# Running the last feed-forward sublayer inside the steps of the cross attention before it, with float32r halves

## The chip, the cores and the metric

The kernel runs on one core of a Trainium2 chip. A core has five engines with a queue of instructions each: TensorE (PE in the profile; PEld is its loading of the stationary operand), VectorE (DVE), ScalarE (ACT), GpSimd (POOL) and SyncE (SP, which here only issues transfers). They run side by side and wait for each other with semaphores. The metric is the device time of one execution in microseconds; three executions of the kernel before are shown below.

## The reference

A decoder of four layers works on 64 sequences of 64 tokens with 256 channels, 4096 tokens in all. Each layer has three sublayers (self attention, a cross sublayer, a feed-forward), each followed by `x = layernorm(x + sublayer(x))`. The change concerns the last layer:

```python
x = _layernorm(x + _L3_attn_ref(x, ...))        # sublayer 10: 16 heads of 128
x = _layernorm(x + _L3_xattn_ref(x, ctx, ...))  # sublayer 11: 16 query heads, 4 key/value heads
x = _layernorm(x + _L3_ffn_ref(x, w_fc, w_proj))  # sublayer 12

def bitlinear(x, w):
    xn = layer_norm(x)                  # eps 1e-6
    x_hat = clip(xn * 128 / max|xn|, -128 + eps, 128 - eps) * max|xn| / 128
    w_hat = sign(round(w / (mean|w| + eps))) * mean|w|     # ternary weights
    return x_hat @ w_hat.T
ffn(x) = bitlinear(gelu(bitlinear(x, w_fc)), w_proj)       # 256 -> 1024 -> 256
```

The weights of the twelfth sublayer are thus -1, 0 or 1 times one number per matrix.

## The kernel before

All tokens stay in SBUF: eight groups `X[g]` of four tiles (`TG = 4`) of 128 tokens by 256 channels, in float32. Beside them stand eight buffers `CT[g]` of the same size that hold the turned context until the cross attention has used it. Large weights go through a ring of eight buffers. PSUM is divided into banks with names: "mm" (two banks in the attentions; the products "p" come there), "tr" (two banks, for every group of up to four transposes, `transpose4`), "s", "y" and "acc".

Sublayers 10 and 11 are one loop (`l3_attentions`, L1870). Its items are 64 for the self attention and 64 for the cross attention, two (`hb` = 0, 1: half of the heads) for each of the 32 token tiles. A step `i` works on item `i` and finishes earlier ones: it projects the queries of item i, turns the queries and keys of item i-1 and makes its scores, takes the softmax rows of item i-2 through a transpose to the product with the values, and multiplies item i-3 by the output matrix. The order of PE's instructions is that of the code (`manual_schedule` for PE). The order on the other engines and the issue of transfers is set by a planner, which simulates the program with its own costs. In the cross attention the order of PE in a step is: turned query 0 of item i-1, query 0, turned key, turned query 1, outputs of item i-3 (L2274, 16 instructions), scores of item i-1 (L2223, 32), turned softmax rows of item i-2, query 1, and for some tiles the values' projection, then values of item i-2 (L2255). On even steps of 14 of the 32 tiles keys and values are loaded from memory, where they have been written earlier (`ContextRows`); for the other 18 they are projected in the step.

The tiles of x are turned (tokens to the free axis) for the projections by whole groups: four transposes and one copy of 512 columns for each half of the channels (`transposed`, `rows`, L2287). The row's end of the cross attention (`tile_normalized`, L360 to L367) finishes x tile by tile, three items after its queries.

Sublayer 12 (`l3_ffn`) is a stage of its own behind the loop. Its weights are made ternary ahead of it (`ternary`, L2315 to L2326, on DVE and POOL), during the cross attention. The normalised and clipped rows of a group (`l3_quantized`, L2337 to L2354) go to `CT[g]`; the first two groups are made near the end of the cross attention. Per tile: `hidden` (L2398, four float32 products of 512 columns, then Gelu L2402 on ACT and the normalisation of 1024 columns on DVE, POOL and ACT), `turned` (eight transposes, two copies, L2412), `output` (L2419, eight float32 products of 256 columns, then the sum with x and the last layernorm). The transposition of a tile stands two to three steps behind its hidden products. The 32 tiles are stored at the end of the program (L479), each once it is final.

Gelu, Exp and Silu need different tables in ACT; where the function changes to one whose table is not loaded, the program has an instruction ACT_TABLE_LOAD.

## Time and profile before

| what | value |
|---|---|
| time, median of 3 runs | 4254.79 us |
| lowest and highest of them | 4251.92 and 4256.56 us |
| span of the profiled execution, first to last instruction | 4250.0 us |
| mean granted TensorE clock | 0.986 |
| scores of the self attention, L2004, first and last start | 1903.2 and 3149.3 us |
| scores of the cross attention, L2223, first and last start | 3174.2 and 3949.7 us |
| last product of the cross attention's output, end | 3963.8 us |
| feed-forward, from there to the end | 286.2 us |

The profile's own execution has no time besides its span; the median of the runs is 4.8 us above that span. In a line of groups the columns are the source line, the engine, the operation, what is written and read with its form, the number of instructions, their busy time in us, the mean of one in ns, and the idle time of the engine just before them with what ended it. The durations of PE's products are longer than the distance of their starts, because they are pipelined; the distance of starts is the pace.

### The profile page before, as it was taken

To read this page: it belongs to the slowest core of one execution; us is meant where nothing else is said; L and a number is where in the kernel's file an instruction comes from. 1 tells how busy PE (TensorE), PEld (TensorE's weight loads), DVE (VectorE), ACT (ScalarE), POOL (GpSimd) and SP (SyncE) were. 2 spreads that over 40 slices of the span, in tenths; PEclk is the share of its full clock that TensorE was granted. 3 is DMA by queue.
4 is the path that set the end of the run, shared out by engine and by line. 5 is a ranking of instruction groups with operands and counts; after the bars stand their busy time and mean duration, and the time that the engine had idled before them with its cause. 6 is when DMAs were issued, how large, how long until landed. Compare 5 with 4: busy or idle time off the path is not lost.

```text
span 4250.0 us, 74130 instructions
## 1 busy us (share of the span) xinstructions
PE 4051.5 (95%) x28788; PEld 2618.4 (62%) x28808; DVE 3042.7 (72%) x6107; ACT 2106.4 (50%) x3863; POOL 1506.3 (35%) x1553
## 2 busy tenths in 40 slices
PE   8889999989998999989999999999999999999998
PEld 5645556666675555546666666666656666666666
DVE  6844548888685688877777777777766777777786
ACT  5555635767634577544444444444433444444443
POOL 4511112242341111115555555555544444444111
PEclk9989999999999999999999999999999999999999
DMA  2200002333300000031111111111131100000000
GB/s 81 73 21 10 1 26 69 72 84 71 82 1 12 1 1 1 10 132 28 26 31 26 26 31 26 26 30 27 26 102 28 26 23 21 23 23 16 11 16 18
DMA packets 108294, 144.00 MB, mean 34 GB/s; under 512 B 15844, under 2 KB 73380, under 8 KB 106536
## 3 DMA queue, kind: packets, MB, share of 16 engines
q1 hardware_dynamic: 106984, 137.69, 12.7%
q8 instruction: 228, 3.74, 0.4%
q10 hardware_dynamic: 960, 1.57, 0.2%
q14 instruction: 122, 1.00, 0.1%
HBM read 70.25 MB, written 26.76 MB: 23 GB/s over the span
## 4 chain that ended last, share of the span: by engine, by line
PE 65%; DVE 15%; ACT 6%; POOL 4%; issue 3%; DMA 1%; SPq 0%; POOLq 0%; ACTq 0%; DVEq 0%
PE p L1777 19%; PE acc L2066 5%; PE acc L2274 4%; PE sq L1208 3%; PE ret L1247 2%; PE qT L319 2%; PE acc L1396 2%; POOL rstd L313 2%; DVE bnst L339 2%; PE gate L911 2%; DVE mc L1213 2%; PE gate L1592 2%; PE sk L1211 2%; PE s L2004 2%; PE up L911 2%
## 5 line engine op out<-in xcount | busy, mean ns | idle before, releaser
L313 POOL TENSOR_TENSOR rstd<-rstd,neg_half 128x1 f32<-128x1 f32 (+1 forms) x195 | 157.9, 810 | 653.1 <-DVE rstd L311 585.2
L313 POOL TENSOR_TENSOR hrq<-hrq,neg_half 128x4 f32<-128x4 f32 x256 | 258.7, 1011 | 300.7 <-DVE hrq L311 283.9
L1213 DVE TENSOR_REDUCE mc<-sq 128x2 f32<-128x512 f32 x512 | 317.1, 682 | 63.9 <-PE sk L1211 63.7
L1219 ACT ACTIVATE e<-sk 128x512 f32<-128x512 f32 x512 | 265.5, 608 | 112.1 <-PE sk L1211 111.5
L1208 PE MATMUL sq<-l1x 32*128 32x256 f32 x2048 | 275.2, 407 | 4.9 <-DVE z L1094 3.1
L1777 PE MATMUL p<-l3a_wq,xt 128*128 128x512 f32 x512 | 243.8, 599 | 11.2 <-DVE v L300 9.9
L313 POOL TENSOR_TENSOR hrk<-hrk,neg_half 128x4 f32<-128x4 f32 x160 | 188.2, 1176 | 185.8 <-DVE hrk L311 181.0
L1211 PE MATMUL sk<-l1x 32*128 32x256 f32 x2048 | 252.9, 392 | 0.0
L1777 PE MATMUL p<-l3a_wk,xt 128*128 128x512 f32 x512 | 247.1, 605 | 0.0
L1208 PEld LDWEIGHTS sq<-l1x 32*128 32x128 f32 x2048 | 208.3, 195 | 58.8 <-issue 23.6
L1777 PE MATMUL p<-l3x_wq,xt 128*128 128x512 f32 x512 | 242.3, 596 | 0.3 <-DVE k L2168 0.3
L1777 PE MATMUL p<-l3a_wv,xt 128*128 128x512 f32 x512 | 233.9, 599 | 0.4 <-ACT y L94 0.4
L2274 PE MATMUL acc<-l3x_wo,yt 128*128 128x256 f32 x1024 | 232.4, 380 | 1.6 <-DVE yt L300 1.0
L2066 PE MATMUL acc<-l3a_wproj,yt 128*128 128x256 f32 x1024 | 232.0, 379 | 0.5 <-DVE yt L300 0.5
L2066 PEld LDWEIGHTS acc<-l3a_wproj,yt 128*128 128x128 f32 x1024 | 194.2, 190 | 53.7 <-issue 29.2
L2274 PEld LDWEIGHTS acc<-l3x_wo,yt 128*128 128x128 f32 x1024 | 190.5, 190 | 33.9 <-issue 7.7
L1211 PEld LDWEIGHTS sk<-l1x 32*128 32x128 f32 x2048 | 188.5, 187 | 7.3 <-issue 2.9
L2237 POOL TENSOR_TENSOR s<-s,smx 128x512 f32<-128x512 f32 x64 | 66.9, 1046 | 333.8 <-DVE smx L2236 319.8
L319 PEld LDWEIGHTS qT<-ident,q 128*128 128x128 f32 x1024 | 121.9, 141 | 95.9 <-issue 75.2
L2050 POOL TENSOR_TENSOR hry<-hry,neg_half 128x8 f32<-128x8 f32 x64 | 106.2, 1659 | 183.4 <-DVE hry L2046 183.4
L319 PE MATMUL qT<-ident,q 128*128 128x128 f32 x1024 | 157.4, 277 | 3.3 <-ACT qT L2208 2.4
L1247 PE MATMUL ret<-e,vt 128*32 128x256 f32 x2048 | 140.6, 390 | 18.2 <-DVE mc L1213 17.2
(415 smaller groups left out, 10209.4 us busy)
## 6 DMA issues: line engine op xcount, KB each, us to landing
vs<-v SPq DMA_DIRECT2D x308, 128.0 KB
l3x_kv<-kv SPq DMA_DIRECT2D x28, 256.0 KB
x<-in_x SPq DMA_DIRECT2D x8, 512.0 KB
ct<-in_ctxT SPq DMA_DIRECT2D x8, 512.0 KB
cn<-in_ctx SPq DMA_DIRECT2D x8, 512.0 KB
l1x<-in_ctx SPq DMA_DIRECT2D x128, 32.0 KB
l1x_x<-x SPq DMA_DIRECT2D x8, 512.0 KB
l1x<-l1x_x SPq DMA_DIRECT2D x128, 32.0 KB
```

Source lines behind the costliest of these rows:

```text
L313: nc.gpsimd.tensor_tensor(out, out, self.neg_half[:, :n], ALU.pow)
L319: self.nc.tensor.transpose(ps[:, j * P : (j + 1) * P], blk, self.ident)
L911: nc.tensor.matmul(ps[:n], w[:, c, h0 : h0 + n], xt[:, c, :], start=c == 0, stop=c == 1)
L1208: nc.tensor.matmul(ps[:, n, :], x_[rows, j, part], c_[rows, j, :], start=True, stop=True)
L1211: nc.tensor.matmul(ps[:, n, :], c_[rows, j, part], x_[rows, j, :], start=True, stop=True)
L1213: nc.vector.tensor_reduce(mc[new % 2][:, ra + k, 2 * j : 2 * j + 2], ps, AX.X, ALU.max, negate=True)
L1219: nc.scalar.activation(es[rb + k], ps, AF.Exp, scale=scale)
L1247: nc.tensor.matmul(ret[32 * r : 32 * r + 32, :], vt[i % 2][:, lc, 4 * r + j, :], es[r][:, lc, :], start=lc == 0, stop=lc == 1,)
L1777: self.nc.tensor.matmul(ps, lhs(c), w(c, cols), start=c == 0, stop=c == 1 and bias is None)
L2050: nc.gpsimd.tensor_tensor(r, r, self.neg_half[:, :8], ALU.pow)
L2066: nc.tensor.matmul(acc[:, :D], yts[h % 2][:, h // 2, :], wp[n // 8][:, (n % 8) * D : (n % 8 + 1) * D], start=n == 0, stop=n == 15,)
L2274: nc.tensor.matmul(acc[:, :D], yts[h % 2][:, h // 2, :], w.o[n // 8][:, (n % 8) * D : (n % 8 + 1) * D], start=n == 0, stop=n == 15,)
```

## The change

A new class `L3Ffn` holds the twelfth sublayer as six pieces per tile, and each piece is put into a step of the loop over sublayers 10 and 11. Hidden products of tile k stand in step `max(n + 2k + 7, n + 25 + 4k // 3)` with n = 64: 89, 90, 91, 93, 94, 95, ... up to 127 for k = 28, and then 129, 131 and 133. The rows of a tile are normalised two steps earlier and turned one step earlier; the scales of the hidden rows follow in the same step, their transposition stands at the end of the next one, the output product and the store in the one after it. The loop runs to step 135 instead of 130. The stage `l3_ffn` and its helpers are gone.

The moving rows are split: after a transpose, ACT copies the PSUM bank into a float32r tile (`hi`) and DVE writes the difference into a second one (`lo`). The ternary weights are float32r as well. A float32 product becomes two float32r products that add up in PSUM. The statistics of the hidden rows come from accumulators of Gelu and of two Square activations in place of DVE's batch statistics. Dividing by the maximum and clipping becomes one clip between -max and max (`limited`). The last layernorm is applied on ACT. The weights are loaded in pieces, twice each (for the mean size and for the sign), in steps 71 to 78, two pieces a step. Hidden rows lie in `CT[0]` and `CT[1]`, small rows in `CT[2]`. The hidden and output products take the banks of "mm", and their transposes those of "tr".

Independently of this, x is turned tile by tile in both attentions: two transposes and one ACT copy of 256 columns at the end of every even step, for the tile that starts two steps later.

```diff
+class L3Ffn:
+    def __init__(self, dec, wk, n):
+        tiles = range(dec.n_groups * TG)
+        first = [max(n + 2 * k + 7, n + 25 + 4 * k // 3) for k in tiles]
+        self.last = first[-1] + 2
+        for k, at in zip(tiles, first):
+            for stage, later in (
+                ("rows", -2), ("rows_turned", -1), ("hidden", 0), ("scales", 0), ("turned", 1), ("output", 2)
+            ):
+                self.events.setdefault((stage, at + later), []).append(lambda s=stage, k=k: getattr(self, s)(k))
+        for i, part in enumerate(self.ternary("l3f_wfc", 0) + self.ternary("l3f_wproj", 1)):
+            self.events.setdefault(("weights", n + 7 + i // 2), []).append(part)
...
+        def size(i):
+            nc.vector.tensor_reduce(col[:, i : i + 1], piece(i), AX.X, ALU.add, apply_absolute_value=True)
...
+        def sign(i):
+            raw, thr, out = piece(i), st["thr"], st["w"][:, i * 512 : (i + 1) * 512]
+            nc.vector.tensor_scalar(out, raw, thr[:, 1:2], None, ALU.is_lt)
+            nc.vector.scalar_tensor_tensor(out, raw, thr[:, 0:1], out.bitcast(F32), ALU.is_gt, ALU.subtract)
...
+    def limited(self, x):
+        am = self.dec.small(2, "am")
+        nc.vector.tensor_reduce(am[:, 0:1], x, AX.X, ALU.max, apply_absolute_value=True)
+        nc.vector.tensor_scalar_mul(am[:, 1:2], am[:, 0:1], -1.0)
+        nc.vector.tensor_scalar(x, x, am[:, 0:1], am[:, 1:2], ALU.min, ALU.max)
+    def standard(self, out, x, eps):
...
+        nc.vector.bn_stats(st, x)
+        nc.vector.bn_aggr(mv, st)
+        dec.rsqrt(r, mv[:, 1:2], 1.0, eps)
+        nc.vector.scalar_tensor_tensor(b, mv[:, 0:1], -1.0, r, ALU.mult, ALU.mult)
+        nc.scalar.activation(out, x, AF.Identity, bias=b, scale=r)
+    def halves(self, hi, lo, ps):
+        self.nc.scalar.copy(hi, ps)
+        self.nc.vector.tensor_tensor(lo, ps, hi.bitcast(F32), ALU.subtract)
+    def rows(self, k):
+        self.standard(out, self.dec.X[g][:, t, :], 1e-6)
+        self.limited(out)
+    def rows_turned(self, k):
+        ps = self.dec.transpose4([rows[:, c * P : (c + 1) * P] for c in range(2)], "xt")
+        xs = [wk.tile([P, 2, P], F32R, tag=n, name=n, bufs=1) for n in ("xhi", "xlo")]
+        self.halves(*(x.rearrange("p c n -> p (c n)") for x in xs), ps[:, :D])
+    def hidden(self, k):
+        for i in range(2):
+            ps, cols = dec.bank("h", bufs=2), slice(i * 512, (i + 1) * 512)
+            for c in range(2):
+                for j, x in enumerate(xs):
+                    nc.tensor.matmul(ps, x[:, c, :], w[:, c, cols], start=c + j == 0, stop=c + j == 2)
+            nc.scalar.activation(h[:, cols], ps, AF.Gelu, scale=self.gammas[0], accum_out=col[:, i : i + 1])
+    def scales(self, k):
+        nc.vector.tensor_scalar(nb, col[:, 0:1], col[:, 1:2], -1.0 / self.HID, ALU.add, ALU.mult)
+        for i in range(2):
+            sq = self.wk.tile([P, 512], F32, tag="sq", name="sq")
+            nc.scalar.activation(
+                sq, h[:, i * 512 : (i + 1) * 512], AF.Square, bias=nb, accum_out=ss[:, i : i + 1]
+            )
+        nc.vector.tensor_scalar(r, ss[:, 0:1], ss[:, 1:2], 1e-6 * self.HID, ALU.add, ALU.add)
+        nc.gpsimd.tensor_tensor(r, r, dec.neg_half[:, :1], ALU.pow)
+        nc.vector.tensor_tensor(b, nb, r, ALU.mult)
+        nc.scalar.activation(h, h, AF.Identity, bias=b, scale=r)
+        self.limited(h)
+    def turned(self, k):
+        for i in range(2):
+            ps = self.dec.transpose4([h[:, (4 * i + j) * P : (4 * i + j + 1) * P] for j in range(4)], "ht")
...
+            self.halves(*(x.rearrange("p j t -> p (j t)") for x in hs), ps)
+    def output(self, k):
+        ps = dec.bank("o", bufs=2)
+        for j in range(8):
+            for m in range(2):
+                nc.tensor.matmul(
+                    ps[:, :D], hts[j // 4][m][:, j % 4, :], w[:, j, :], start=j + m == 0, stop=j + m == 8
+                )
+        nc.vector.scalar_tensor_tensor(z, ps[:, :D], self.gammas[1], x, ALU.mult, ALU.add)
+        self.standard(x, z, 1e-5)
+        nc.sync.dma_start(out=dec.out[at : at + P, :], in_=x)
...
@@ l3_attentions @@
-            for i in range(2 * n + 3):
+            for i in range(ffn.last + 1):
...
                     do(0, "query", 0)
+                    ffn.run("output", i)
                     do(1, "key_turned")
                     do(1, "turn", 1)
-
+                    ffn.run("hidden", i)
...
                 while self.row_ends:
                     self.row_ends.pop(0)()
-                if i in (n - 3, n - 2):
-                    two.rows(0, i - n + 3)
+                for stage in ("scales", "weights", "turned", "rows_turned", "rows"):
+                    ffn.run(stage, i)
+                if i % 2 == 0 and i + 2 < 2 * n:
+                    which, j = at(i + 2)
+                    which.rows(j // 2)
...
+    def tile_turned(self, wk, k):
+        ps = self.transpose4([self.X[g][:, t, c * P : (c + 1) * P] for c in range(2)], "xt")
+        xt = wk.tile([P, 2, P], F32, tag="xt", name="xt", bufs=3)
+        self.nc.scalar.copy(xt, ps[:, :D].rearrange("p (c n) -> p c n", c=2))
```

## The prediction

> **What bounds the kernel now.** I read the page first, then the same busy times by stretch, then single rows. The page's head:
>
> ```profile
> PE 4051.5 (95%) x28788; PEld 2618.4 (62%) x28808; DVE 3042.7 (72%) x6107; ACT 2106.4 (50%) x3863; POOL 1506.3 (35%) x1553
> ```
>
> PE leads, but "busy" has modelled ends, so I use busy times only to see where PE stops. The change touches the end of the program: the eleventh sublayer (cross attention, steps 64 to 130 of the loop at L1870, scores at L2223 from 3174.2 to 3949.7 us) and the twelfth (feed-forward, after the last L2274 product at 3963.8 us). The same view by stretch, four attention steps and then the feed-forward (columns: stretch, its length, busy us of PE, PEld, DVE, ACT, POOL):
>
> ```profile
> 3696.41:3744.19 47.78, 47.65 (x358) 32.95 (x357) 35.42 (x68) 19.90 (x35) 20.09 (x21) 1.00 0.10 23
> 3990.00:4230.00 240.00, 224.00 (x940) 153.32 (x938) 189.03 (x531) 110.51 (x170) 40.03 (x60) 1.00 0.05 16
> ```
>
> In the attention PE never stops and four steps (two token tiles) take 47.75 us. DVE has 12 us idle in them, ACT and POOL 28 each. In the feed-forward nobody is full: PE 93%, DVE 79%. Its groups in the stretch 3990 to 4225 (us busy, mean ns, idle before):
>
> ```profile
> L2419 PE MATMUL o<-l3f_wproj,ht 128*128 128x256 f32 x443 | 101.9, 381 | 5.2 <-ACT ht L2412 5.2
> L2348 DVE TENSOR_REDUCE am<-hn 128x1 f32<-128x1024 f32 x28 | 34.1, 1218 | 21.5 <-ACT hn L2342 21.1
> L2342 ACT ACTIVATE hn<-h,nmr,rstd 128x1024 f32<-128x1024 f32 x27 | 33.5, 1240 | 83.2 <-DVE nmr L2337 82.8 <-DVE bnmv L342 0.4
> ```
>
> The idle of ACT is spent on DVE and that of DVE on ACT: one tile's normalisation runs back and forth. The chain of work that ended last agrees: in that stretch it goes through DVE, POOL and ACT, hardly through PE. So 286.2 us (3963.8 to 4250.0) are paid for 32 tiles, 8.9 us each. Pace of PE and price of an ACT table, from the timeline:
>
> ```profile
> 1162.72 0.59 PE L1378 MATMUL gate<-xt,l_signs 128*128 128x512 bf16 x2
> 1163.16 0.59 PE L1378 MATMUL up<-xt,l_signs 128*128 128x512 bf16 x2
> ...
> 4158.80 1.04 PE L319 MATMUL ht<-ident,hn 128*128 128x128 f32 x8
> 4159.67 3.60 PE L2398 MATMUL h<-l3f_wfc,xt 128*128 128x512 f32 x8
> 4163.11 3.62 PE L2419 MATMUL o<-l3f_wproj,ht 128*128 128x256 f32 x16
> ...
> 1502.87 0.47 ACT L1564 ACTIVATE eq<-qk,ss 128x256 f32<-128x256 f32 x1
> 1503.24 0.47 ACT L1566 ACTIVATE wv<-qk,ss 128x256 f32<-128x256 f32 x1
> 1503.73 1.28 ACT L1596 ACT_TABLE_LOAD   x1
> 1505.02 0.60 ACT L1596 ACTIVATE hid<-gate 128x512 f32<-128x512 f32 x1
> ```
>
> A bf16 product of 512 columns is one instruction, 0.216 us from start to start (two in 0.44). One f32 product is two instructions (8 for 4 products in L2398) of (3.60-0.59)/7 = 0.43 us: 0.86 us, four times as much. A transpose costs 0.11.
>
> **The change, part by part.**
>
> *Removed:* the feed-forward as a stage of its own, 286.2 us, with its wait for the attention's last rows and its back-and-forth per tile.
>
> *PE work put into the attention.* Per tile: hidden, 4 products as two float32r halves = 8 instructions of 512 columns; output, 8 products = 16 of 256; transposes 8+2. No row shows float32r. Bounds: the bf16 pace (0.216 per 512 columns, one instruction) and the f32 pace (0.86). I take bf16, because the operand is cut into two halves and each needs no second part, which is what makes f32 two instructions. Then 8 x 0.216 + 16 x 0.108 + 10 x 0.11 = 4.5 us, against 3.6 + 3.6 + 1.3 = 8.5 now. The weight loads of transposes follow each other at the same 0.11, so they do not hold 256 columns back (0.108). The page "FP8 and Floating Point Precision" (TensorE Precision Notes) says that true FP32 takes four passes and that a reduced form reads FP32 cut to FP22; the trace agrees on the factor four, and no run here shows the reduced form; by one pass the estimate is the same 4.5 us.
>
> *The pace of the new steps.* The schedule `first` hides hidden(k) at step 89 + 4k/3, so 3 tiles per 4 steps until step 127: tiles 0 to 28. Floor by PE: 47.75 + 3 x 4.5 = 61.2 us per 4 steps.
>
> Other engines in those 4 steps. DVE per tile: rows 0.40 + 0.17 + 0.15 + 0.16 + about 0.36 (maximum over 256, half of L2145's 0.67) + 0.14 + 0.35; halves of the rows 0.42 (L360); scales 0.15 x 3 + 1.22 + 0.14 + 0.74; halves of the hidden rows 2 x 0.68 (L2168, PSUM, 512); output 0.47 + 0.42 + 0.17 + 0.15 + 0.16: sum 7.5. Group sums overlap: 213 us of them are 189.0 busy in the stretch, so 6.7. DVE: 35.4 + 3 x 6.7 = 55.5, fits under 61.2. ACT per tile: 0.60 + 0.37 + 2 x 0.69 + 2 x 0.63 + 4 x 0.20 (read-outs of accumulators, as L1557) + 1.24 + 2 x 0.58 + 0.60 = 7.4. Gelu and Exp now alternate; Silu and Exp do in the trace, with 1.28 us at every change: two per tile, 2.6. ACT: 19.9 + 3 x 10.0 = 50. POOL: 20 + 3 x 3 x 0.62 = 25.6.
>
> Against this the page "ScalarE: Activation LUTs" (Table sets: the hidden batching unit; What ACT_TABLE_LOAD costs) speaks: batch by set, for a switch costs about 2.66 us, 1.28 and a drain. Here the load starts 0.02 us after the activation before it ends and the next begins at its end, so 1.28 is what this trace supports. By the page ACT would be at 58 of some 67, still under PE.
>
> *Waits added on PE.* They come from order, not from load. At the end of a step `turned` fills both "tr" banks; `rows_turned`, the xt transposes or the next step's qT need the first one again. It comes free only after ACT's copy (0.58) and then DVE's subtraction (0.68), with some 0.15 us between engines: 1.4 us, less 0.43 in which the second bank is filled. That is 1.0 us per tile with both queues empty. DVE has a backlog at the end of a step: at 3774.4 the yt products are done and DVE finishes its copy only at 3775.9, the hrq reduction at 3776.6, so 1 us more. Behind the waiting transpose all of PE's next step waits. Per 4 steps: three such pairs, 3 x 2.0; two refills more by rows and xt, 0.25 each: 6.5 us. Bounds: 0 (queues empty, PE finds the bank free) and 14 (nine bank uses, each behind 1.5 us of backlog). The shared "p" banks add nothing in my sum: hidden falls on steps 1, 2, 3 of four, where query 1 comes 5 us later, behind out, scores and pt.
>
> So 67.7 us per 4 steps, 20 more than now, 6.65 per tile; 29 tiles: **+193 us**.
>
> *The tail.* The last three tiles stand at steps 129, 131 and 133 with PE nearly idle: a chain of latencies. From the last L2274 product: row's end 2.8 (3963.8 to 3966.6 now); behind it tile 30's output, hidden, scales (squares 1.3, pow 0.6, identity 1.24, maximum 1.22, clip 0.9, hops) and turning, to about 18; tile 31's hidden 1.7, gelu 1.5, scales 6.3, turning 0.9, copies 1.4, output 1.8, z to x 2.5 (4244.9 to 4247.4 now), store 2.5: **+36 us**, bounds 28 and 45.
>
> *With one answer, nothing:* **Rows turned tile by tile** in both attentions: the same 8 transposes per group, ACT 4 x 0.37 instead of 2 x 0.58, covered by ACT's 28 idle us in 48; were ACT full, 16 groups x 0.3 = 5 us. Its bank was last read 3 us earlier (q and value products lie between); bounds -5 (no lump of 8 at a group's end) and +15. **Ternary weights**: 16 pieces at steps 71 to 78 with DVE 8 x 0.68 + 8 x (0.36 + 0.95) = 16 us, against 2 x 2.28 + 8 x 0.95 on DVE and 8 x 1.57 on POOL at 3174 to 3621 now, in the same steps with 12 us of DVE idle per four. Its 16 loads of 256 KB and the 32 stores pass SP ahead of vs and k, v loads; the queue moves 23 GB/s, and vs is needed two steps later. A store that waits for x holds SP some 5 us of a 17 us step. **POOL's** three pows per tile (0.62) stand before hrq and s, which have over 4 us of slack. **l3_prepare** leaves the attention: 48.4 instead of 47.75 in two fours, -1.4.
>
> **Sum:** 3963.8 + 193 + 36 - 1.4 = 4191 us of span, against 4250.0; with the 4.8 us by which the median of the runs (4254.8) exceeds the profiled span: **4195 us**, -1.4%.
>
> **Rivals.**
>
> *A, PE packs almost without waits:* the pairs cost at most 0.7 us per tile. For it: ACT and DVE have idle time, and now PE loses only some 2 us in four steps. Against it: one bank pair for all. 4195 - 29 x (1.5 to 2.17): 4132 to 4152.
>
> *B, slower: the "tr" banks hold PE.* Place: the end of the step, T0/T1 then rows, xt, qT. For it: DVE at 55.5 of 61, in order, with waits for ACT's tables and POOL's pows inside it. Margin to the old time: 60 us / 29 tiles = 2.07 us; so it decides from 4.2 us of wait per tile (12.7 per four steps, 74 us long). At 14 to 18: 4267 to 4305.
>
> *C, float32r is no faster than f32 per column:* 10 us more per tile at the full f32 price (+297, about 4500), 3.4 at half of it (4295). Nothing in the trace excludes it; the one-instruction bf16 rows are nearer. It decides from 1.6 times the bf16 pace.
>
> *D, no gain kept:* the steps get longer by what the stage saved, 73 to 75 us per four: 4246 to 4263.
>
> **How the numbers follow.** The likeliest, 4160 to 4235 us: 0.60. A: 0.21. Sum of losses between, B 0.10, C 0.05, D 0.04. A measurement of this kernel can tell about 0.2% (8.5 us) from no change, so D is "same": faster 0.81, same 0.04, slower 0.15. The range 4125 to 4265 holds A, the likeliest and D and leaves out B and C; on one side only the packing is better.
>
> **What would show it.** Right: L2223's starts per four steps go from 47.75 to about 68 after step 88 and are unchanged before; the new products on PE start 0.216 and 0.108 apart; some 60 ACT table loads of 1.28 appear between Gelu and Exp; PE idles before transposes at the end of steps, released by the DVE subtraction; under 40 us follow the last L2274 product. Wrong: float32r rows as pairs or at 0.43; steps of 74 us; waits of PE in "p" products on Gelu; a longer self-attention (scores L2004, 19.8 us a step); or DVE idle while waiting for ACT, with PE waiting for DVE.

## The result: slower, 4405 us instead of 4256

Measured side by side, the changed kernel takes 4405.3 us (median of 4 runs, 4399.3 to 4407.3), the kernel before 4255.7 (4 runs): a ratio of 1.035, 95% interval 1.0335 to 1.0365. The prediction was 4195, with 0.15 on slower. The direction was wrong and the time lies outside the range. The profiled execution of the changed kernel spans 4397.3 us at a mean granted clock of 0.960; before, 4250.0 at 0.986.

### The profile after

The page's head (busy us, share of the span, instructions) and its row of the granted TensorE clock, in 40 slices of 110 us:

```profile
PE 4036.5 (92%) x28788; PEld 2623.1 (60%) x28808; DVE 3020.5 (69%) x6139; ACT 2265.4 (52%) x4200; POOL 1500.8 (34%) x1569
PEclk9989999999999999999999999999999988888898
```

PE's and DVE's busy time hardly changed, and yet the span grew by 147 us. From slice 33 on, where the feed-forward runs inside the steps, the clock reads 8 (80 to 90%) instead of 9. The same four-step stretch that was shown for before (47.78 us, PE 47.65 busy, clock 1.00) now has the feed-forward in it; two in a row, with the same columns:

```profile
3863.20:3951.98 88.78, 72.11 (x460) 50.81 (x459) 54.49 (x132) 47.67 (x85) 25.11 (x29) 0.87 0.06 17
3951.98:4040.70 88.72, 72.06 (x461) 50.76 (x460) 54.45 (x132) 47.64 (x85) 25.11 (x29) 0.87 0.06 17
```

Four steps take 88.7 us, not the forecast 67.7. The loads are what the prediction worked out (DVE 54.5 for 55.5, ACT 47.6 for 50, POOL 25.1 for 25.6), and no engine is full: PE itself is idle for 16.7 us of them, and its clock is 0.87.

Where the 147 us lie, by the starts of the scores and the last output product:

| stretch | before, us | after, us | difference | predicted |
|---|---|---|---|---|
| up to step 87 | 3456.3 | 3465.9 | +9.6 | -1.4 |
| steps 87 to 128 | 492.5 | 865.2 | +372.7 | +193 |
| scores of step 128 to the end of the last output product | 15.0 | 24.6 | +9.6 | 0 |
| behind it | 286.2 | 41.6 | -244.6 | 36 us left (-250) |

The rows sum to +147.3. The second one is the case.

**What PE waits for.** One end of a step from the timelines of PE, ACT, DVE and POOL, in order of time (start, us, engine, line, what, and in brackets the idle time before it with its releaser). L492 are transposes, L374 the subtraction that makes the low half, L373 the copy that makes the high half, L413 the squares and L416 to L419 the rest of the scales of the *next* tile; L2413 (exponential), L2323 and L471 on ACT belong to the attention:

```profile
3956.45 1.09 PE L492 MATMUL ht<-ident,ct 128*128 128x128 f32 x8
3958.09 0.63 ACT L2413 ACTIVATE s<-s 128x512 f32<-128x512 f32 x1
3958.76 0.63 ACT L2323 ACTIVATE sq<-q 128x512 f32<-128x512 f32 x1
3959.29 0.57 ACT L471 COPY yt<-y 128x512 f32<-128x512 f32 x1
...
3960.48 0.72 ACT L413 ACTIVATE sq<-ct,hcol 128x512 f32<-128x512 f32 x1
...
3961.20 1.05 ACT L373 CAST hhi<-ht 128x512 fp32r<-128x512 f32 x2
3961.33 0.21 DVE L416 TENSOR_SCALAR hcol<-hcol 128x1 f32<-128x1 f32 x1 [0.68 <-ACT sq L413]
3962.69 0.55 POOL L417 TENSOR_TENSOR hcol<-hcol,neg_half 128x1 f32<-128x1 f32 x1
3963.27 0.16 DVE L418 TENSOR_TENSOR hcol<-hcol 128x1 f32<-128x1 f32 x1 [1.73 <-POOL hcol L417]
3963.35 1.28 DVE L374 TENSOR_TENSOR hlo<-ht,hhi 128x512 fp32r<-128x512 f32 x2
...
3964.09 0.69 PE L492 MATMUL xt<-ident,ct 128*128 128x128 f32 x2 [6.54 <-DVE hlo L374]
```

The eight transposes have filled both transpose banks at 3957.5. The copy out of them needs 1.05 us on ACT, and it starts only at 3961.2: ahead of it in ACT's queue stand 2.2 us of the attention (the exponential, a square and the copy of y, until 3959.8) and then 1.4 us of squares of the next tile. The subtraction needs 1.28 us on DVE, and it starts only at 3963.35, because the next tile's L418 stands ahead of it in DVE's queue and waits there 1.73 us for a power on POOL. DVE stood idle in this wait although the first half of the copy was done by 3961.8, so it worked its queue off in order. The code runs the stage `scales` of one tile before `turned` of the tile ahead of it. Of the 6.5 us for which PE stands here, the scales thus make about 3 (an estimate from these rows: 1.4 on ACT, 1.6 on DVE); the attention's own work and the two copies are the rest. A four has three such ends of a step, with waits of 6.5, 5.6 and 2.3 us. Over the whole execution PE's transposes lose 136 us to this one instruction (waits: who, for whom, us in total, times, longest):

```profile
PE xt L492 <- DVE hlo L374: 86.3, 29, 6.6
PE qT L492 <- DVE hlo L374: 49.6, 9, 5.6
```

**What the wait does to the clock.** Behind such a wait, from PE's timeline:

```profile
3901.25 1.12 PE L492 MATMUL qT<-ident,q 128*128 128x128 f32 x4 [5.63 <-DVE hlo L374]
3902.16 3.62 PE L1946 MATMUL p<-l3x_wkv,ct 128*128 128x512 f32 x4
3905.57 2.31 PE L1946 MATMUL p<-l3x_wq,xt 128*128 128x512 f32 x4
...
3910.00 1.88 PE L1946 MATMUL p<-l3x_wq,xt 128*128 128x512 f32 x4
```

Four instructions of this form (two float32 products of 512 columns) take 3.62 us behind the wait and 1.88 us eight us later. So a wait of 5.6 us costs about another 2.2 us (3.62 + 2.31 instead of 2 x 1.88). The page "TensorE: Matmul & The Clock Gate" of the Trainium skill (Why this matters for your kernels) says it as a rule: no gap of PE over some 3 us, else the clock falls to half until PE has been busy for about 4 us. The trace agrees in size: after gaps of 5.6 and 6.5 us half pace, after one of 1.07 us none. In this kernel short gaps close together went with it too: behind 2.26, 0.23 and 0.46 us, with nothing but transposes between, four such instructions took 3.62 us again.

So 88.7 us are 62.1 (the floor, with the measured pace of the new products) + 16.7 idle + a remainder of about 10, which is put down to the slow clock (an estimate; the second experiment tests it).

### The profile page after: what moved, and what is told of

Same layout as the page of the kernel before. It is cut to its first block, busy times and chain, and to the rows that moved or that the text cites. A ratio compares the mean times of both kernels' runs of the same rounds, so it can differ in the third digit from the quotient of the medians.

```text
span 4397.3 us, 74354 instructions
## 1 busy us (share of the span) xinstructions
PE 4036.5 (92%) x28788; PEld 2623.1 (60%) x28808; DVE 3020.5 (69%) x6139; ACT 2265.4 (52%) x4200; POOL 1500.8 (34%) x1569
## 4 chain that ended last, share of the span: by engine, by line
PE 63%; DVE 17%; ACT 6%; POOL 4%; issue 2%; DMA 1%; SPq 0%; DVEq 0%; POOLq 0%; ACTq 0%
PE p L1946 19%; PE acc L2246 5%; PE acc L2453 4%; PE sq L1377 2%; PE qT L492 2%; PE ret L1416 2%; PE acc L1565 2%; DVE mc L1382 2%; PE gate L1080 2%; PE o L442 2%; PE gate L1761 2%; PE s L2184 2%; PE sk L1380 2%; PE up L1080 2%; PE up L1761 1%
## 5 line engine op out<-in xcount | busy, mean ns | idle before, releaser
L1382 DVE TENSOR_REDUCE mc<-sq 128x2 f32<-128x512 f32 x512 | 317.2, 682 | 61.0 <-PE sk L1380 60.7
L486 POOL TENSOR_TENSOR rstd<-rstd,neg_half 128x1 f32<-128x1 f32 (+1 forms) x187 | 148.3, 797 | 461.0 <-DVE rstd L484 445.3
L1946 PE MATMUL p<-l3x_wq,xt 128*128 128x512 f32 x512 | 276.0, 666 | 0.4 <-DVE k L2347 0.3
L492 PE MATMUL qT<-ident,q 128*128 128x128 f32 x1024 | 169.4, 292 | 70.3 <-DVE hlo L374 49.6
L492 PEld LDWEIGHTS qT<-ident,q 128*128 128x128 f32 x1024 | 129.8, 149 | 163.9 <-issue 71.0
L1946 PEld LDWEIGHTS p<-l3a_wv,xt 128*128 128x128 f32 x512 | 91.1, 190 | 112.4 <-issue 80.8
```

What stands on the lines that cost most here:

```text
L486: nc.gpsimd.tensor_tensor(out, out, self.neg_half[:, :n], ALU.pow)
L492: self.nc.tensor.transpose(ps[:, j * P : (j + 1) * P], blk, self.ident)
L1382: nc.vector.tensor_reduce(mc[new % 2][:, ra + k, 2 * j : 2 * j + 2], ps, AX.X, ALU.max, negate=True)
L1946: self.nc.tensor.matmul(ps, lhs(c), w(c, cols), start=c == 0, stop=c == 1 and bias is None)
```

## The experiments

The theory after this reading, Q: PE waits for the place that the copies of the turned tile have in the queues of ACT and DVE, and the slow clock follows from the waits. Its rivals: the new products themselves slow the clock; the halves' work on DVE is too much; the changes of ACT's table hold ACT up; the two transpose banks are too few (rival B of the prediction).

The times of before that belong to them are 4252 to 4254 us. "A four" is the time of four steps of the eleventh sublayer with three tiles of the feed-forward in them. e2, e3, e4, e5, e8, e13 and e14 are one execution each; four executions of e1 lie between 4316.5 and 4345.6 us.

| run | what | us | a four, us | clock in it |
|---|---|---|---|---|
| after | | 4405.3 | 88.7 | 0.87 |
| e1_order | turned before scales | 4327.2 | 78.4 | 0.93 |
| e2_warm | after, PE kept busy | 4363.1 | 81.3 to 85.9 | 0.94 to 1.00 |
| e3_tiles | before, rows turned tile by tile | 4267.9 | | |
| e4_onetable | e1, no table changes | 4315.5 | 78.4 | 0.93 |
| e5_f32 | after, without halves | 4422.7 | 87.9 to 89.6 | 0.92 to 0.94 |
| e6_place | turned in the middle of the step | 4340.3 | 81.9 | |
| e7_weights | e6, weights over more buffers | 4336.8 | | |
| e8_parity | e3, the other copy engine | 4282.1 | | |
| e9_halves | before, halves alone | 4234.5 | | |
| e10_free | e1, bank freed by one ACT copy | 4354.5 | 81.9 | 0.92 |
| e11_later | e9, output one tile later | 4215.1 | | |
| e12_bank | e1, one bank elsewhere | 4312.3 | 78.5 | 0.91 |
| e13_banks | e1, both banks elsewhere | 4292.6 | 76.9 | 0.91 to 0.93 |
| e14_mid | e6, all turning in mid-step | 4387.8 | 85.3 | |

### 1. The order alone: e1_order

```diff
-                for stage in ("scales", "weights", "turned", "rows_turned", "rows"):
+                for stage in ("turned", "rows_turned", "scales", "weights", "rows"):
```

> Edit: at the end of a step the turning of the hidden rows (with its ACT copies and DVE subtractions) is issued before the scales of the next tile, not after them; nothing else moves. Theory Q (queue order: the subtraction that frees the tr bank stands on DVE behind a scales chain that waits for ACT squares and a POOL pow): PE's idle in four steps falls from 16.6 us to 6 or less, the granted clock there goes from 0.87 back over 0.97, four steps take 66 to 70 us instead of 88.7, the time is 4180 to 4240 us. Theory S (the two banks and the two copies themselves are too slow, whatever the order): four steps stay over 86 us, the time stays over 4370 us.

4327.2 us (ratio to before 1.0188, 1.0157 to 1.0218): one line of order is worth 78 us, a four falls by 10.3 us. So the part of the reading that concerns the order is shown: the other tile's scales stood in front of the copies. But half of the expected gain is missing, and neither expectation was met. A four of it:

```profile
3891.08:3969.51 78.43, 67.32 (x459) 47.90 (x459) 52.89 (x131) 47.08 (x84) 25.48 (x29) 0.93 0.07 19
```

The longest of its waits in twelve steps, and two of the three ends of a step in a four:

```profile
PE xt L492 <- DVE hlo L374: 23.3, 9, 5.3
...
3915.65 0.69 PE L492 MATMUL xt<-ident,ct 128*128 128x128 f32 x2 [5.26 <-DVE hlo L374]
3935.95 0.70 PE L492 MATMUL qT<-ident,q 128*128 128x128 f32 x4 [1.78 <-DVE hlo L374]
```

The gain lies in the second of them (1.8 for 5.6 us); the one that was shown above hardly changed (5.3 for 6.5), and the third not at all (2.3). Idle time falls by 5.6 us per four, and the rest of the 10.3 is put down to the clock (0.93 for 0.87). At the first end the copy still starts 3.9 us behind the transposes. One of the next tile's squares (0.8 us with the read-out of its sum) is still in front of it, for the planner sets ACT's order, then the table change (1.28), the attention's exponential and a copy; DVE's row sum waits for the exponential with the subtraction behind it.

### 2. The clock by itself: e2_warm

The order of after; behind each turned tile PE gets 20 (at one tile of three 8) useless float32r products of 512 columns, which nothing reads: 48 x 0.23, 11 us of PE work more in a four.

```diff
+        for j in range(n if k <= 28 else 0):
+            self.nc.tensor.matmul(ps, w1[:, 0, :P], w0[:, 0, :512], start=True, stop=True)
```

> Edit: behind the turning of the hidden rows PE gets 20 products of 512 columns without a use (8 on every fourth step), 0.234 us each, into the bank of the scores; the order of all else stays. They fill the time in which PE waits for the subtraction. Theory K (the clock falls because PE stands idle for some 3 us or more at the end of a step, and that costs 10 of the 27 us that four steps have over their floor): granted clock in the stretch over 0.97, four steps 78 to 82 us, time 4300 to 4340 us, although PE has 11 us more work in four steps. Theory P (the float32r products themselves lower the clock): clock stays at 0.87 or below, time 4390 to 4500 us.

Two fours of it:

```profile
3920.27:4001.57 81.30, 74.95 (x507) 55.05 (x506) 53.97 (x131) 47.57 (x84) 25.14 (x29) 1.00 0.06 19
4001.57:4085.10 83.53, 77.14 (x497) 55.39 (x497) 53.88 (x130) 46.02 (x81) 25.13 (x29) 0.94 0.06 17
```

More work, and 42 us less time (4363.1 for 4405.3), with the clock back at 1.00 in the first four. So the low clock comes from PE's gaps and not from the new kind of product, and it is worth about the 5 us by which a four got shorter (83.6 on the mean). That is Theory K, with less gain than it asked (4300 to 4340 us). About half of the remainder of 10 us is shown by this; PE still idles 6.3 us in these fours.

### 3. What the halves are worth in the steps: e5_f32

The sublayer in its new place, but with whole float32 rows: no halves, no subtraction on DVE.

```diff
-            self.halves(*(x.rearrange("p j t -> p (j t)") for x in hs), ps)
+            self.nc.scalar.copy(hs.rearrange("p j t -> p (j t)"), ps)
...
-            for m in range(2):
-                nc.tensor.matmul(
-                    ps[:, :D], hts[j // 4][m][:, j % 4, :], w[:, j, :], start=j + m == 0, stop=j + m == 8
-                )
+            nc.tensor.matmul(ps[:, :D], hts[j // 4][:, j % 4, :], w[:, j, :], start=j == 0, stop=j == 7)
```

> Edit: the changed kernel without the halves: rows and hidden rows are copied once by ACT as float32 and multiplied as float32, DVE subtracts nothing. PE gets 3.7 us more per tile (8.5 instead of 4.8), its floor in four steps is 73.3 us. Theory Q: the banks come free with ACT's copy, PE waits 3 to 6 us in four steps, clock over 0.95, 77 to 83 us in four steps instead of 88.7, time 4280 to 4350 us. Theory S: the wait stays as it is and 29 times 3.7 us come on top, about 4500 us.

4422.7 us, 17 more than after and between the two expectations; one four:

```profile
3950.32:4038.26 87.94, 76.98 (x460) 51.45 (x459) 48.33 (x122) 47.59 (x84) 24.93 (x29) 0.94 0.06 17
```

PE has about 9.5 us more to do per four (3 x 3.2: eight products of 256 columns and four of 512 take 6.9 us a tile as float32 here, and 3.7 in halves), and the four is no longer than with halves (88.6 on the mean); what remains of the waits now names ACT's copy. So in the steps the halves bring nearly nothing: what the products gain is lost again in idle time (16.7 us for 11.0 here) and in the slow clock (0.87 for 0.94). The subtraction alone is not the cause either, for without it PE waits for the copy before it.

### 4. The table changes: e4_onetable

The first experiment with Square in place of Gelu, so that ACT never changes tables in these steps (the activation function is not computed).

```diff
-            nc.scalar.activation(h[:, cols], ps, AF.Gelu, scale=self.gammas[0], accum_out=col[:, i : i + 1])
+            nc.scalar.activation(h[:, cols], ps, AF.Square, scale=self.gammas[0], accum_out=col[:, i : i + 1])
```

> Edit: the reordered kernel of the first experiment, with Square in place of Gelu (the output is not the reference's), so that ACT never changes its table in the steps; the count and the size of ACT's instructions stay. Theory T (what still holds the subtraction back after the reordering is the softmax's Exp with its table load of 1.28 us ahead of it on ACT, with DVE's row sums waiting for it): the waits of PE on the subtraction in four steps fall from 9.5 us by 3 to 6 us, with the clock behind them 5 to 9 us in all, time 4315 - 50 to 90, 4225 to 4265 us. Rival (tables lie in ACT's idle time and cost nothing, as my prediction had it): within 15 us of the first experiment's 4315.

A four is 78.4 us with and without the changes: ACT's busy time falls from 47 to 39 us in it, the waits of xt on hlo shorten (18.0 for 23.3 us in twelve steps) and nearly as much appears at other places (products waiting for DVE's copy of q, 4.9 for 0.9). In this order the table changes cost the time nothing.

### 5. Another place in the step: e6_place, e14_mid

e6: the turning one step later, in the middle of the step before the hidden products, which move ahead of the turned key with it; the output one step later too. e14: the turning of the rows moved there as well.

```diff
-                ("rows", -2), ("rows_turned", -1), ("hidden", 0), ("scales", 0), ("turned", 1), ("output", 2)
+                ("rows", -2), ("rows_turned", -1), ("hidden", 0), ("scales", 0), ("turned", 2), ("output", 3)
...
+                    ffn.run("turned", i)
+                    ffn.run("hidden", i)
...
-                for stage in ("scales", "weights", "turned", "rows_turned", "rows"):
+                for stage in ("rows_turned", "scales", "weights", "rows"):
```

and e14 against e6:

```diff
                     ffn.run("hidden", i)
+                    ffn.run("rows_turned", i)
...
-                for stage in ("rows_turned", "scales", "weights", "rows"):
+                for stage in ("scales", "weights", "rows"):
```

> Edit: the turning of a tile's hidden rows stands in the second step after its hidden products, between the output product of the tile before and the hidden products of a later tile, so that PE has 1.9 us of other work before it needs one of the two banks again; the output follows one step later. Work is the same. Theory Q: PE hardly waits for the subtraction, clock over 0.98, four steps 63 to 68 us, 4190 to 4235 us in all, faster than the kernel before. Theory S (DVE and ACT together cannot serve two banks in time): four steps over 74 us, over 4270.

> The sixth experiment (hidden rows turned one step later, in the middle of the step before the hidden products), with the turning of the tile's rows moved there too, behind the hidden products; banks as they were. Nothing of the sublayer is turned at the end of a step any more. Theory R (the wait is long where ACT and DVE are held by the softmax, at the end of the step): the waits of qT on xlo (19 of 41 us in that run's twelve steps) go, 72 to 77 us per four steps instead of 81.9, 4265 to 4310 us. Rival M (any place in the step has some queue in front of it): the waits come back as waits of other transposes on hlo or xlo, 80 to 84, 4325 to 4345.

e6: 4340.3 us (1.0203, 1.0185 to 1.022), a four 81.9; its longest waits are now those of qT for the rows' low half (19.0 us in twelve steps) and for hlo (16.1). Theory Q (4190 to 4235) failed here; the result is Theory S's. e14: 4387.8 us, worse than e6, a four 85.3, and the waits have moved again. Both of its expectations were too low; the one that said "any place has some queue in front of it" is the nearer. Two of its waits, from PE's timeline:

```profile
3961.64 1.14 PE L492 MATMUL ht<-ident,ct 128*128 128x128 f32 x8 [2.59 <-ACT xt L2115]
...
3989.54 0.69 PE L492 MATMUL xt<-ident,ct 128*128 128x128 f32 x2 [5.37 <-DVE hlo L374]
```

### 6. The banks: e10_free, e12_bank, e13_banks

Rival B had put the blame on the two "tr" banks. All three have the order of e1. e10 empties a bank with one ACT copy, the halves are made from that by ACT and POOL. e12 takes the first of the two hidden banks from the scores, e13 the second one from the products too; no instruction is added in them.

```diff
-        self.nc.scalar.copy(hi, ps)
-        self.nc.vector.tensor_tensor(lo, ps, hi.bitcast(F32), ALU.subtract)
...
+        self.nc.scalar.copy(raw, ps)
+        self.nc.scalar.copy(hi, raw)
+        self.nc.gpsimd.tensor_tensor(lo, raw, hi.bitcast(F32), ALU.subtract)
```

and e13 (e12 has the first pair alone):

```diff
-            ps = self.dec.transpose4([h[:, (4 * i + j) * P : (4 * i + j + 1) * P] for j in range(4)], "ht")
+            ps = self.dec.transpose4([h[:, (4 * i + j) * P : (4 * i + j + 1) * P] for j in range(4)], "ht", *(("s", 1), ("mm", 2))[i])
```

> The order of the first experiment, and the turned tiles are copied out of their bank once, by ACT, to SBUF; hi is then made by ACT and lo by POOL from that copy. So the bank waits for no DVE instruction and comes free one ACT copy earlier; DVE is relieved of 5 us per four steps, ACT gets 4 and POOL 8 more. Theory Q (PE waits for the place of the subtraction in DVE's queue): the waits of transposes on hlo vanish (23 of 33 us idle in twelve steps), idle falls from 11 to 5 to 7 us per four steps, the clock rises, and a four takes 70 to 73 us instead of 78.4: 4250 to 4285 us median. Rival R (any engine's queue is late there, ACT's as well): the transposes wait for ACT's copy instead, 76 to 79 us per four, 4310 to 4335. Rival P (POOL becomes the late one: its lo behind s, pows and k in its queue): output products wait for hlo, four steps over 80.

> The order of the first experiment, with the first of the two banks of a tile's turned hidden rows taken from the scores' bank, which is free at the end of a step, instead of the two shared transpose banks; nothing else changes, no instruction is added or removed. Theory B (the two shared banks couple PE's next transposes to the late subtraction): one shared bank stays free for the rows' and the next step's transposes, idle falls from 11 to 4 to 7 us per four steps, the clock rises from 0.93, a four takes 69 to 73 us instead of 78.4: 4245 to 4285 us. Rival R (the waits are for the data, not for the bank: the output products and the next transposes need what the same queues bring late): 76 to 79 us per four, 4310 to 4335.

> The order of the first experiment; the turned hidden rows use the scores' bank and one of the products' two banks, and no shared transpose bank. No instruction is added. Theory B (the shared transpose banks are the cause): PE's wait of 5.3 us before the transposes goes and nothing takes its place, 68 to 73 us per four steps instead of 78.4, 4225 to 4285 us. Rival R (ACT and DVE work off their queues in order, and what PE needs next stands in them behind the exponentials and the halves): the transposes go early, and PE waits instead for ACT's copy of the turned rows, or for the half in the rows' bank; 75 to 79 us per four, 4295 to 4330.

e10: 4354.5 us (1.0232, 1.0215 to 1.0249), a four 81.9, slower than e1. The waits on DVE's hlo are gone; in twelve steps PE now waits 15.0 us for ACT's raw copy, as R had it, and 9.0 us for POOL's low half of the rows; the size is P's.

e12: 4312.3 us (1.014, 1.0125 to 1.0155), a little under the runs of e1 (4316.5 to 4345.6), and a four is the same 78.5. Transposes wait for hlo six times in twelve steps instead of twelve, and 29.6 us instead of 28.6 (xt and qT together): the second bank holds PE in place of the first. That agrees with R's numbers, but it still is a bank that PE waits for.

e13: 4292.6 us; its four of 76.9 us lies in R's range, the whole between B's upper end (4285) and R's lower one (4295). What took the bank's place, in order of time from the timelines of PE and ACT:

```profile
3900.18 0.38 PE L492 MATMUL xt<-ident,x 128*128 128x128 f32 x2
...
3901.72 1.28 ACT L2413 ACT_TABLE_LOAD   x1
...
3904.02 1.08 ACT L373 CAST hhi<-ht 128x512 fp32r<-128x512 f32 x2
...
3905.24 0.75 ACT L413 ACTIVATE sq<-ct,hcol 128x512 f32<-128x512 f32 x1
...
3905.95 0.39 ACT L2113 COPY xt<-xt 128x256 f32<-128x256 f32 x1
3906.40 1.12 PE L492 MATMUL qT<-ident,q 128*128 128x128 f32 x4 [5.83 <-ACT xt L2113]
```

PE turns the attention's rows at 3900.2, 1.2 us behind the start of the hidden rows instead of 7 as in e1, and then waits 5.8 us for ACT to copy them: 0.39 us of work that stands behind the exponential, the copies of the hidden rows and a square. The waiting transposes don't need these rows: they turn q, which DVE had written by 3900.3 (L2347), and the copied rows are for a tile that starts two steps later. So they wait for a "tr" bank again, now held by the rows of x, and they do so for 27.3 us in twelve steps, hardly less than the 28.6 of e1. What holds PE is a pair: a bank, and a copy out of it that stands, on engines that are 60 to 70% busy (ACT 46 and DVE 53 of 77 us), behind work that PE doesn't need yet. e1 shows the queue's share. How much would go with more banks for all transposes stays open; no run here has them.

### 7. The tile-by-tile turning: e3_tiles, e8_parity

The kernel before, with only this part of the change; e8 also swaps which of ACT and DVE takes the alternating copies.

```diff
-                if i in (n - 3, n - 2):
-                    two.rows(0, i - n + 3)
+                if i % 2 == 0 and i + 2 < 2 * n:
+                    which, j = at(i + 2)
+                    which.rows(j // 2)
```

and e8 against e3, once at the start of the self-attention:

```diff
+                self.turn ^= 1
```

> Edit: the kernel before with only the turning of x tile by tile in both attentions. My reading (it is free): within 8 us of the kernel before, scores of step 65 within 8 us of 3174. Rival (it is what makes the changed kernel 5.6 us late at step 65 and 9.6 us late at step 87): 4262 to 4275 us.

> Edit: the kernel before with x turned tile by tile, as in the third experiment, with the alternation of copies between ACT and DVE shifted by one, as it was before (the removed copy at the start had shifted it). Theory V (the 15 us come from the shifted alternation): 4250 to 4257 us. Theory A (they come from the turning itself, its transposes and ACT copies in every second step): 4264 to 4270 us.

e3: 4267.9 us, 15 more than before (the rival's range), nearly all of it in the self-attention (first to last start of its scores 1261.6 us instead of 1246.1). The wait of PE that grew most there, in e3:

```profile
PE yt L319 <- ACT kT L1771: 10.7, 8, 1.5
```

and in the kernel before:

```profile
PE yt L319 <- ACT kT L1771: 4.3, 9, 0.5
```

That is 6 of the 15 us; a new wait of xt for DVE's xq is 3.6 more. Swapping the copies makes it worse (4282.1, outside both expectations), so the old alternation doesn't bring the 15 us back, and the rest of them is not explained. In the changed kernel itself the self-attention takes 1256.5 us, 10 more than before.

### 8. The weights: e7_weights

e6 with the pieces of the weights going through four buffers instead of two, seven steps later.

```diff
-            self.events.setdefault(("weights", n + 7 + i // 2), []).append(part)
+            self.events.setdefault(("weights", n + 14 + i // 2), []).append(part)
...
-            raw = dec.CT[0][:, i % 2, :]
+            raw = dec.CT[i // 2 % 2][:, i % 2, :]
```

> Edit: the one before, and the weight pieces go through four buffers instead of two (CT[0] and CT[1]), seven steps later. Theory: DVE waits for fewer transfers in its queue; the 10 to 14 us that steps 70 to 73 are longer than in the kernel before shrink to 4 or less: 6 to 12 us faster than the one before. Rival: the cost is DVE's own work of 16 us and comes again in the later steps: within 4 us.

4336.8 us (1.0198, 1.0181 to 1.0215), 3.5 less than e6. Steps 70 to 73 return to their old length, and steps 77 to 80 get longer instead; steps 65 to 87 take 283.9 us for 286.2. So the cost of 10 to 12 us moves along with the pieces, as the rival had it.

### 9. The halves without the move: e9_halves, e11_later

The kernel before with its feed-forward as a stage of its own, and the products in halves there, with the scales from ACT's sums, as in the change. The weights are made ternary through other buffers, and the first group is turned at the start of the stage. e11: PE's output products of a tile come one tile later still.

```diff
-                    nc.tensor.matmul(
-                        ps, xt[:, c, t * P : (t + 1) * P], wfc[:, c, i * 512 : (i + 1) * 512],
-                        start=c == 0, stop=c == 1,
-                    )
+                    for j, x in enumerate(groups[g]):
+                        nc.tensor.matmul(
+                            ps, x[:, c, t * P : (t + 1) * P], wfc[:, c, i * 512 : (i + 1) * 512],
+                            start=c + j == 0, stop=c + j == 2,
+                        )
```

and e11 against e9:

```diff
-                if i >= 3:
-                    output(*tiles[i - 3], hts.pop(i - 3))
+                if i >= 4:
+                    output(*tiles[i - 4], hts.pop(i - 4))
```

> The kernel before, with its feed-forward left as a stage of its own, and in it only the rows and hidden rows as two float32r halves (and the scales from ACT's sums instead of the two statistics on DVE). Theory H (the halves are a gain by themselves; what cost the time was putting the work between the steps of the attention): the tile's PE work falls from 8.5 to 4.5 to 4.8 us, DVE carries some 6.3 and ACT 6.5 to 7, so a tile takes 7.2 to 7.6 us instead of 8.9; the part after the last L2274 product falls from 286 to 230 to 245 us and the median lies at 4195 to 4215 us. Rival G (the clock: with PE full to two thirds only, its gaps halve the clock here too): granted clock 0.85 to 0.95 in the stage, tiles at 7.8 to 8.6, 4220 to 4245. Rival L (one tile's chain of latencies sets the pace, whatever PE takes): 8.7 to 9.0 per tile, 4248 to 4258.

> The separate stage with halves (ninth experiment), with each tile's output products one tile later on PE, so that a whole tile of work lies between its turning and them. There a tile took 8.0 us with PE 7.2, DVE 7.8 of ten busy, and PE's main wait was the output product for hlo (30 of 230 us). Theory Q (PE's waits are for copies that stand late in DVE's queue, so distance takes them away): these waits go, the clock returns to 0.97 to 1.00, a tile takes 7.1 to 7.6 us: 4205 to 4225 us median. Rival D (DVE with what waits in its order is the bound): the waits move to the transposes and the hidden products, 7.9 to 8.1 per tile, 4230 to 4238.

e9 takes 4234.5 us (0.9956, 0.9941 to 0.997): the change's arithmetic is a gain where the stage was. A tile takes 8.0 us, more than theory H asked; rival G, the clock, has the numbers. 200 us of its stage:

```profile
3990.00:4190.00 200.00, 145.02 (x836) 124.27 (x835) 158.55 (x439) 147.44 (x318) 32.28 (x54) 0.91 0.05 16
```

e11 takes 4215.1 us (0.9914, 0.9897 to 0.993): 0.9% faster than before and 4.3% faster than the change. The same stretch of it:

```profile
3990.00:4190.00 200.00, 152.86 (x971) 131.60 (x969) 176.58 (x497) 166.75 (x360) 37.68 (x64) 0.95 0.06 19
```

PE gets through 971 instructions in 200 us instead of 836. The 28.2 us that e9's output products waited for hlo are gone. The stage, counted from the end of the last attention product, takes 239 us (e9 256, before 286), 7.5 us a tile: the time is Q's. The waits are partly D's, for transposes now wait 43 us for the low halves, and DVE, busy for 177 of 200 us, is nearest to being the bound. In the attention both kernels lose 8 to 16 us against before on balance: the two steps in which the weights are made ternary (94 and 102) take 17 to 19 us more, and steps 65 to 87 some 8 to 9 less.

## Why the prediction was wrong

- **The floor, 61.2 us per four: right.** The new products were forecast 0.216 and 0.108 us apart. They are 0.11 and 0.23 us apart, each one instruction, as PE's timeline of after shows below. The floor is 62.1, and rival C falls.
- **DVE 55.5, ACT 50, POOL 25.6 per four: right** (54.5, 47.6, 25.1), and with that the sentence that order, not load, makes the waits.
- **"Waits added on PE ... 6.5 us", bounds 0 and 14: this step failed.** It took 1.0 us of wait per tile with empty queues and 1 us of backlog. Measured: 16.7 us idle per four, above the upper bound. The backlog was priced from DVE's work at the end of a step in the kernel before, and two things were left out. One is what the change itself puts into the queues ahead of the copy: the scales of the next tile, which the diff's list of stages shows in front of `turned` (e1: 10.3 us of the 21 missing per four, 5.6 of them idle time), with a DVE instruction that waits for POOL among them. The other is ACT's own backlog, 2.2 us of the attention in the step shown above; in e1 the copy there still starts 3.9 us behind the transposes. The place was named rightly: transposes at the end of a step, released by the subtraction.
- **The slow clock was in no term.** With the sum's own method 16.7 us idle make 4290 us of span (4191 + 10.2 x 29/3); about 10 us more per four remain, and e2 shows 5 of them to be the clock. The profile of before could hardly show it, since PE never stopped in these steps there.
- **Rival B had the sign, the place and the wait, not the size.** Its 14 to 18 us of wait per four hold the 16.7 measured; it ended at 4305 for want of the clock. Its reason, the "tr" banks, is half of the matter: PE does wait for them, in e13 too, but the order of ACT's and DVE's queues alone is worth 78 us (e1).
- **"ACT table loads", covered: right.** 59 of them, forecast some 60, each 1.28 us; taking them away changes nothing in the order of e1 (e4). The next activation starts at the load's end (3901.72 + 1.28, and the exponential at 3903.02), so the drain that the page "ScalarE: Activation LUTs" of the Trainium skill (What ACT_TABLE_LOAD costs) adds to a load is not seen here.
- **Rows turned tile by tile, "nothing", bounds -5 and 15: mis-sized.** 15 in e3, at the bound; about 10 in the changed kernel. The cover named, ACT's idle time, didn't hold: the wait that grew most is PE's for a copy on ACT (10.7 for 4.3 us).
- **Ternary weights, "nothing": mis-sized.** Steps 70 to 73 take 12 us more (60.7 for 48.4), which DVE's idle 12 us per four were to cover. Steps 65 to 87 together take 4 more on balance, since the kernel before pays for its own weights there (e9 and e11, which make theirs later, take 8 to 9 less than it).
- **The tail, 36 us: 41.6, inside its bounds.** PE waits in it twice for a tile's scales (8.8 and 8.4 us), as listed. The last stretch before it costs another 9.6 us, which was not in the sum.

The new products in after:

```profile
3909.34 0.28 PE L442 MATMUL o<-l3f_wproj,hhi 128*128 128x256 f32 x1
3909.45 0.28 PE L442 MATMUL o<-l3f_wproj,hlo 128*128 128x256 f32 x1
...
4359.83 0.40 PE L401 MATMUL h<-l3f_wfc,xlo 128*128 128x512 f32 x1
4360.06 0.39 PE L401 MATMUL h<-l3f_wfc,xhi 128*128 128x512 f32 x1
```

Counted against the sum: steps 87 to 128 +180, before them +11, last steps +9.6, tail +5.6: 206 us, from 4191 to 4397 of span.

## What to carry to other kernels

Before work is put into the gaps of engines that are half idle, write down for each engine what stands in its queue ahead of the one instruction that PE will wait for, the moved work's own instructions included: 54 of 89 us busy tells nothing of how late a 1.3 us copy comes. Steps in which PE was never idle show no clock loss in the profile before (1.00 here), and the gaps that a change makes there can cost more than their length: here 16.7 us idle and about 10 more. Ask also what a waiting transpose waits for, its data or a bank, and whose copy empties that bank. Where a faster form of the products and a move come together, price and run them apart: here the form alone, in the old place with one tile more of distance, is the gain (4215 us), and the move loses it.

## What the runs showed of the hardware

- Two float32r products on halves of the rows are nearly as fast as the bf16 rows would suggest: 0.23 us per 512 columns and 0.11 per 256, one instruction each, against 0.86 for the whole f32 product in two instructions. That is a factor of 1.8 for the two halves together, 3.2 us a tile.
- PE's clock pays for gaps: behind 5.6 us of idle the next 3.6 us run at half pace, and 11 us of useless products per four made the kernel 42 us faster.
- A change of ACT's table, 1.28 us, twice per tile, cost no time at all in the order of e1 (e4), though ACT stood in the chain of waits: when it went, another queue was the late one.
